# A sparse two-layer graph network on one core: the last chunk's loads before a copy, and layer 0's loop recut

## The chip, the cores and the metric

The kernel runs on one core of a Trainium2 chip. The core has five engines that work side by side, each through its own list of instructions in order: PE (matrix products), DVE (vector operations), ACT (scalar functions and copies), POOL (here it issues the gathers and scatters) and SP (here it issues plain transfers). Semaphores make one engine wait for another. Transfers of all of them run on 16 DMA engines. The metric is the device time in microseconds (us) of one execution; lower is better.

## The reference, cut to what matters

There are N = 3327 nodes with 512 features each, and a symmetric 0/1 adjacency matrix with ones on its diagonal, in which a row holds few ones. Two layers follow one another:

```python
# layer 0: attention with 4 heads of 128
feats = einsum('nf,hfo->hno', x, W)
logits = leaky(e_self[:, None] + e_neigh[None, :], 0.2)      # only where adj is 1
x = layernorm(x + relu(softmax(logits) @ feats + b))
# layer 1: a gated sum of an attention over x @ W_sa and a plain sum over x @ W_gcnb
a = exp(-leaky(s_left[:, None] + s_right[None, :], 0.01)) * adj
x = layernorm(x + sigmoid(gate_a * (a / a.sum(1)) @ (x @ W_sa) + gate_b * (adj @ (x @ W_g) + b_g)))
```

## The kernel before, in words

The kernel never forms the dense attention. It reads the adjacency matrix once, turns each row into a list of neighbours, sorts the nodes by their number of neighbours, and then gathers the feature rows of the neighbours. Nodes are worked on in tiles of 128, 26 of them: 12 in a first group, 14 in a second. `CAPS` gives the neighbours of each tile, its own node apart (14 down to 5, and 14 down to 4). The two tiles with the longest lists (`T0`, tiles 0 and 12) have a further row of shared slots, the stairs.

**Loading.** The matrix comes in seven chunks of 512 columns, the last of 256. SP issues the loads in the order of the program: 13 blocks of a chunk (`load_adj`, line 222, into 12 rotating buffers), then a chunk of x (`load_x`). Ahead of the last chunk's 13 blocks SP issues `x_rows` (line 238), a copy within HBM of the first group's x rows into `table0`, beside the place of their features, so that one gather brings a node's x and its features together. Two more copies of that kind, for the second group (`own1`, lines 989 and 990), are issued later in the program and stand next in SP's list.

For each chunk, PE sums the blocks into codes (`add_codes`, line 403), ACT takes them out of PSUM (`take_codes`), PE turns them (`turn_codes`), and DVE draws the lists from them with top-eight operations (`top_codes`, `decode`, `pick`). Between these, `features` multiplies x by the weights of layer 0 and POOL writes the rows to `table0`.

**Layer 0.** Gathers go into a ring of 42 slots (`RING`). `plan` gives each row of each tile of `order0` its slot; `gather` (line 616 through `indirect`) issues, on POOL, the gathers for which slots are free by the program's count. A gather waits for the readers of the old row in its slot. `order0` begins with tiles 11, 10, 0, 1, 2; the two first are short (6 and 7 rows). For each tile:

- `weigh_a` and `weigh_b` compute the softmax weights of its rows, on DVE and ACT. They need all its gathers.
- `attend` multiplies each row by its weights, one per head, and adds it up on PE in the accumulator `acc` by a product with the identity (line 804). Rows whose number leaves 2 after division by 3 are multiplied by ACT in four pieces (line 796), the others by DVE (line 798). From the fourth tile on (`lean`) the bias is added to row 0 on DVE (line 803); otherwise PE adds it (line 790).
- `finish` takes the accumulator, adds x (line 883, DVE), and frees the tile's slots.
- `columns1` turns the tile on PE, `columns2a` copies that on ACT, `columns2` multiplies it on PE by eight columns that layer 1 needs, `columns3` copies the result on DVE (line 839).
- `norm.add` takes statistics on DVE; for each group of up to four tiles `publish` writes the normalised rows to `table1`.

In the order of the program tiles 11 and 10 (`early`) are weighed before the last chunk's codes are summed, and multiplied and added up right after that. The other 24 tiles are in a loop. In its iteration i an engine's list holds: publishing that is due; the copy of tile i-2's turned columns; the rows of tile i, multiplied and added up, with the eight columns of tile i-2 on PE after the third row; the finishing of tile i-1, its turning and statistics; the column copy of tile i-2; two of the 14 steps that sort the second group (`sort1`) while these last; the weights of tile i+1.

**Layer 1** follows with a loop of its own over gathers from `table1`; the change doesn't touch it.

Of the kernel before, what the change touches and what calls it, by code (L numbers as in the profile page):

```python
# [14 lines left out]
P = 128  # L15
# [63 lines left out]
def sparse_pass(  # L79
# [156 lines left out]
    for i in range(len(chunks)):  # L236
        if i == len(chunks) - 1:
            x_rows = nc.sync.dma_start(twos.rearrange("(n t) w -> n t w", t=2)[:, 0, :], xo[:N0]).ins
            tc.add_to_no_dep_group("x rows", x_rows)
        load_adj(i)  # L240
        load_x(i + 2)

# [301 lines left out]
    def sort1(to, t0, t1):  # L544
# [16 lines left out]
        if t1 == n:  # L561
            by_tile = in_place[0].rearrange("p (t w) -> p t w", t=n)
            nc.vector.tensor_copy(srt[1][:, :, : S + 2], by_tile[:, :, : S + 2])
            nc.vector.tensor_copy(srt[1][:, :, S + 2 : W1].bitcast(F32), by_tile[:, :, S + 2 :])
# [34 lines left out]
    def climb(g, pool, psum):  # L599

        of = pool.tile([P, B + H], F32, tag="of", name=f"of{g}")
        nc.vector.tensor_copy(of[:, :B], srt[g][:, 0, C0 + 1 : S + 1])
        nc.vector.tensor_copy(of[:, B:], srt[g][:, 0, S + 2 : S + 2 + H].bitcast(F32))
        nc.tensor.matmul(psum, to_row, of, start=True, stop=True)
        nc.vector.tensor_mul(of[:, :B], psum[:, :B], step_of)
        id_ = pool.tile([P, 1], F32, tag="id_", name=f"id_{g}")
        nc.vector.tensor_reduce(id_, of[:, :B], AX.X, ALU.add)
        nc.vector.tensor_copy(ids2[g], id_)
        nc.vector.tensor_copy(es2[g], psum[:, B:])
# [134 lines left out]
    def weigh_a(j):  # L744
# [6 lines left out]
        if j in T0:  # L751
            logit = m0.tile([P, H], F32, tag="logit", name=f"logit{j}")
            nc.vector.tensor_add(logit, stair[j][:, F : F + H], es2[g])
            small = psx.tile([P, B * H], F32, tag="pcol", name=f"to_nodes{j}", bufs=2)
# [19 lines left out]
    def weigh_b(j):  # L774
# [5 lines left out]
        if j in T0:  # L780
            small = psx.tile([P, B * H], F32, tag="pcol", name=f"to_rows{j}", bufs=2)
            ws2[j] = to_rows(m0, small, f"n{j}", w[:, C0 + 1 :, :])

    def attend(j, lean, between):


        w = ws[j]
        acc = accs[j] = ps.tile([P, F], F32, tag="acc", name=f"acc{j}", bufs=2)
        if not lean:
            nc.tensor.matmul(acc, ident, bias0, start=True, stop=False)  # L790
        for s0, n, buf, o in got[j]:
            for s in range(s0, s0 + n):
                gv = buf[:, o + s - s0, 0:F].rearrange("p (h o) -> p h o", h=H)
                if s % 3 == 2:
# [6 lines left out]
                row = buf[:, o + s - s0, 0:F]  # L801
                if lean and s == 0:
                    nc.vector.tensor_add(row, row, bias0)
                nc.tensor.matmul(  # L804
                    acc, ident, row, start=(lean and s == 0), stop=(s == CAPS[j] and j not in T0)
                )
                if s == 2:
                    between()
        if j in T0:
# [4 lines left out]
            nc.tensor.matmul(acc, to_node, stair[j][:, 0:F], start=False, stop=True)  # L814

# [54 lines left out]
    early = order0[:2]  # L872

    def at_first():

        a, b = (CAPS[j] + 1 for j in early)
        waiting[: a + b] = waiting[1:a] + waiting[a + 1 : a + b] + [waiting[0], waiting[a]]
        for _ in range(a + b - 2):
            tc.declare_no_dep(indirect(*waiting.pop(0)[1:]), group="x rows", reason="they read rows of features only")
# [11 lines left out]
    for i in range(len(chunks)):  # L891
        if i == len(chunks) - 1:
# [5 lines left out]
            for j in early:  # L898
                weigh_a(j)
                weigh_b(j)  # L900
        add_codes(i)
        if i == len(chunks) - 1:
            for j in early:
                attend(j, False, lambda: None)
        take_codes(i)
        if i == len(chunks) - 1:
            for j in early:
                finish(j)
# [5 lines left out]
        if i == NC0 + 2:  # L914
            climb(0, p0, psl.tile([P, CH], F32, tag="pc1", name="climb0")[:, : B + H])
# [29 lines left out]
    weigh_a(order0[2])  # L945
    weigh_b(order0[2])
    ready = [[], []]
    for i in range(NT + 3):
# [3 lines left out]
        third = order0[i - 2] if 2 <= i < NT + 2 else None  # L952
        if third is not None:
            columns2a(third)
        if 2 <= i < NT:
            attend(order0[i], i >= 3, lambda: third is None or columns2(third))
        elif third is not None:
            columns2(third)
        if 0 < i <= NT:
            j = order0[i - 1]  # L960
            y = row1(j)[:, 0:F]
            if i > 2:
                finish(j)
            if not waiting:
                put_rows()
            columns1(j)
            done = norm.add(i - 1, y)
            if done:
                k0, scale, shift = done
                ready[1] = [  # L970
                    (order0[k], scale[:, k - k0 : k - k0 + 1], shift[:, k - k0 : k - k0 + 1]) for k in range(k0, i)
                ]
        if i > NT:
            put_rows()
        if 2 <= i < NT + 2:
            columns3(order0[i - 2])
        if 0 < i <= 7:
            sort1(rankis[1], 2 * i - 2, 2 * i)
        if i == 8:
            climb(1, m0, psx.tile([P, B * H], F32, tag="pcol", name="climb1", bufs=2)[:, : B + H])  # L980
# [10 lines left out]
        if 2 <= i < NT - 1:  # L991
            weigh_a(order0[i + 1])
            weigh_b(order0[i + 1])
# [658 lines left out]
```

## Time and profile before

| | |
|---|---|
| median of three runs | 940.53 us (937.54 to 941.17) |
| the profiled execution, as timed | 1068.62 us |
| its span, first to last instruction | 1066.8 us |
| mean granted clock of PE | 0.865 |
| busy PE, DVE, ACT, POOL | 814.2, 735.3, 289.0, 593.5 us |
| moved by DMA | 224.68 MB, 211 GB/s on average |

The profile is of one execution, which took longer than those without a profile; durations in it are those of that execution. A group of instructions is shown as source line, engine, operation and `out<-in` with its shape and count, then its busy time, the mean of one in ns, and how long its engine stood idle ahead of it, with what ended most of that idle time (`<-`). In stretches of the span, "clock" is the share of PE's full clock that was granted, and the DMA share is the mean busy share of the 16 DMA engines. A product of 512 columns in fp32 shows as two matmul records. "remote" or "unknown" stands where the trace shows no releaser.

### The profile page before, as it was taken

The page shows a single profiled execution, that of the slowest core. Times are in us where ns is not written, and L with a number is a line of the kernel's source. Part 1 is how long each engine was busy: PE and PEld are TensorE (multiplying, and loading weights), DVE is VectorE, ACT ScalarE, POOL GpSimd, SP SyncE. Part 2 cuts the span into 40 slices and gives each one's busy share as a digit, 9 for nine tenths or more (in the row PEclk, how much of TensorE's full clock was granted, in tenths as well). Part 3 has the DMA queues.
Part 4 walks back from the last instruction along what each step waited for, and adds up shares of the span by engine and source line. Part 5 has one row for each costly group of instructions (what it writes and reads, how often), then busy time and mean ns, then how long its engine had stood idle before and what let it go on. Part 6 is the DMA issues. An engine that isn't in the chain of part 4 may idle for free. (4 is left out here: it accounts for less than half of the span.)

```text
span 1066.8 us, 10313 instructions
## 1 busy us (share of the span) xinstructions
PE 814.2 (76%) x2518; PEld 426.4 (40%) x2518; DVE 735.3 (69%) x2100; ACT 289.0 (27%) x820; POOL 593.5 (56%) x641
## 2 busy tenths in 40 slices
PE   5698972521987877777987956639999999969993
PEld 4476751201443433333443422214444444434441
DVE  3486788407857467655756757348798998989973
ACT  1122220200424243432434422112323123232331
POOL 7511243760566666465766247765667777757611
PEclk9898995565898879788987977769999999989997
DMA  9999899991477668586676127755656666746400
GB/s 341 371 361 399 342 325 351 377 386 53 126 212 235 199 192 251 144 307 197 183 210 198 61 98 196 207 164 140 188 144 186 183 182 182 195 129 182 167 28 35
DMA packets 73349, 224.68 MB, mean 211 GB/s; under 512 B 12736, under 2 KB 16784, under 8 KB 72384
## 3 DMA queue, kind: packets, MB, share of 16 engines
q0 software_dynamic: 46368, 153.69, 48.8%
q1 hardware_dynamic: 24256, 68.13, 16.8%
q10 hardware_dynamic: 2656, 2.10, 0.6%
q8 instruction: 23, 0.38, 0.1%
q14 instruction: 46, 0.38, 0.1%
HBM read 203.02 MB, written 31.51 MB: 220 GB/s over the span
## 5 line engine op out<-in xcount | busy, mean ns | idle before, releaser
L616 POOL DMA_INDIRECT ring<-table,srt x464 | 475.2, 1024 | 265.1 <-issue 98.8
L804 PE MATMUL acc<-ring,ident 128*128 128x512 f32 x504 | 261.9, 667 | 56.6 <-ACT ring L796 18.5
L1097 DVE SCALAR_TENSOR_TENSOR sw<-ring,e,sw 128x512 f32<-128x512 f32 x226 | 169.4, 750 | 11.6 <-ACT sw L1081 4.7
L804 PEld LDWEIGHTS acc<-ring,ident 128*128 128x128 f32 x504 | 101.7, 212 | 178.8 <-issue 109.2
L1118 PE MATMUL acc<-ring,ident 128*128 128x512 f32 x264 | 126.4, 613 | 13.8 <-DMA ring<-table,srt 9.7
L372 PE MATMUL pf<-w,xc 128*128 128x260 f32 x416 | 105.3, 417 | 13.1 <-DVE w L312 13.1
L798 DVE TENSOR_TENSOR ring<-ring,w 128x512 f32<-128x512 f32 x176 | 111.3, 691 | 1.7 <-DVE w L779 1.2
L1137 PE MATMUL po<-wsa,sT 128*128 128x512 f32 x208 | 98.4, 617 | 18.5 <-ACT sT L1130 10.3
L372 PEld LDWEIGHTS pf<-w,xc 128*128 128x128 f32 x416 | 85.8, 209 | 30.1 <-DVE w L312 13.8
L1137 PE MATMUL po<-wg,sT 128*128 128x512 f32 x208 | 93.8, 593 | 0.8 <-issue 0.8
L796 ACT ACTIVATE ring<-ring,w 128x128 f32<-128x128 f32 x304 | 91.5, 389 | 0.0
L1118 PEld LDWEIGHTS acc<-ring,ident 128*128 128x128 f32 x264 | 50.7, 194 | 81.8 <-issue 54.7
L1137 PEld LDWEIGHTS po<-wsa,sT 128*128 128x128 f32 x208 | 40.9, 199 | 73.4 <-issue 59.3
L1099 DVE TENSOR_TENSOR ring<-ring 128x512 f32<-128x512 f32 x94 | 65.0, 692 | 3.2
L403 PE MATMUL pc<-at,pow 128*32 128x512 bf16 (+1 forms) x182 | 24.6, 414 | 53.0 <-DMA at<-in_adjB 24.4
L384 POOL DMA_DIRECT2D table<-row x26 | 14.3, 549 | 87.2 <-ACT st L381 84.6
L763 ACT ACTIVATE w<-w 128x40 f32<-128x40 f32 (+10 forms) x26 | 6.2, 237 | 201.5 <-DVE w L762 124.8
L1137 PEld LDWEIGHTS po<-wg,sT 128*128 128x128 f32 x208 | 39.3, 190 | 49.9 <-issue 49.7
L1130 ACT COPY sT<-pt 128x512 f32<-128x512 f32 x52 | 28.7, 587 | 102.0 <-remote 48.8
L376 ACT COPY row<-pf 128x512 f32<-128x512 f32 x26 | 15.2, 585 | 96.2 <-PE pf L372 50.6
L829 ACT COPY xt<-x1t 128x512 f32<-128x512 f32 x26 | 15.2, 584 | 94.9 <-remote 39.2
L835 PEld LDWEIGHTS pcol<-v,xt 128*128 128x128 f32 x208 | 33.1, 228 | 17.3 <-issue 14.1
(254 smaller groups left out, 941.7 us busy)
## 6 DMA issues: line engine op xcount, KB each, us to landing
at<-in_adjB SPq DMA_DIRECT2D x78, 512.0 KB
ring<-table,srt POOLq DMA_INDIRECT x464
table<-row POOLq DMA_DIRECT2D x26, 260.0 KB
xc<-in_xB SPq DMA_DIRECT2D x6, 1024.0 KB
own<-in_xo SPq DMA_DIRECT2D x1, 3640.0 KB
own<-table SPq DMA_DIRECT2D x1, 3640.0 KB
at<-in_adjL SPq DMA_DIRECT2D x13, 256.0 KB
table<-in_xo SPq DMA_DIRECT2D x1, 3120.0 KB
```

Of the source, the lines that this page charges most:

```text
L372: nc.tensor.matmul(pf[:, hh, :HC], xc[:, k, o : o + P], w0[:, k, hh, :], start=(k == 0), stop=(k == KT - 1))
L403: nc.tensor.matmul(pc[32 * c : 32 * c + 32, : nt * P], pow2[:, s, :], loaded[i, m], start=(s == 0), stop=(m + 1 not in ms or s == 3),)
L616: return nc.gpsimd.indirect_dma_start(out=out_, out_offset=None, in_=table, in_offset=bass.IndirectOffsetOnAxis(ap=ap, axis=0)).ins
L796: nc.scalar.activation(gv[:, h, :], gv[:, h, :], AF.Copy, scale=w[:, s, h : h + 1])
L798: nc.vector.tensor_tensor(gv, gv, w[:, s, :].rearrange("p (h o) -> p h o", o=1).to_broadcast([P, H, FO]), ALU.mult)
L804: nc.tensor.matmul(acc, ident, row, start=(lean and s == 0), stop=(s == CAPS[j] and j not in T0))
L835: nc.tensor.matmul(pcol, xt1[:, k, :], v1[:, k, :], start=(k == 0), stop=(k == KT - 1))
L1097: nc.vector.scalar_tensor_tensor(sw, g[:, i, 0:F], e[:, s : s + 1], sw, ALU.mult, ALU.add)
L1099: nc.vector.tensor_add(g[:, i, 0:F], g[:, i - 1, 0:F], g[:, i, 0:F])
L1118: nc.tensor.matmul(plain[j], to, row, start=(not sums_of_two and i == 0), stop=(sums_of_two and i == len(rows) - 1),)
L1130: nc.scalar.copy(sT, pt)
L1137: nc.tensor.matmul(proj[j], sT[:, k, :], wt[:, k, :], start=(half + k == 0), stop=(half + k == KT))
```

## The change

It has two parts.

The loads: `x_rows` is issued after the last chunk's loads rather than before. Tiles 11 and 10 are no longer worked on inside the last chunk. `at_first` now issues the gathers of three tiles' rows (11, 10 and 0) that hold features only, 26 of them where there were 11, and then the three tiles' own rows, which wait for the copy.

The loop: it now runs over all 26 tiles. `attend` is cut into `multiply` (DVE and ACT) and `add_up` (PE). In an iteration the list is: the products of tile i; the weights of tile i+1, if its rows fit in the ring beside those not yet freed; the sums of tile i; finishing, turning and statistics of tile i-1; the weights of i+1 if they were not yet done; the columns of tile i-2; the column copy of tile i-3; publishing; sorting. In `lean` tiles rows 0 and 1 are multiplied by four operations each, one per head, that add the bias to row 0, and row 0 to row 1; PE then adds up one row fewer. `climb`, which prepares the stairs, is in two halves an iteration apart for the second group, and small PSUM tiles have a bank of their own (`aux`).

```diff
     for i in range(len(chunks)):
-        if i == len(chunks) - 1:
-            x_rows = nc.sync.dma_start(twos.rearrange("(n t) w -> n t w", t=2)[:, 0, :], xo[:N0]).ins
-            tc.add_to_no_dep_group("x rows", x_rows)
         load_adj(i)
         load_x(i + 2)
+    x_rows = nc.sync.dma_start(twos.rearrange("(n t) w -> n t w", t=2)[:, 0, :], xo[:N0]).ins
+    tc.add_to_no_dep_group("x rows", x_rows)
...
-    def attend(j, lean, between):
+    def multiply(j, lean):
         w = ws[j]
-        acc = accs[j] = ps.tile([P, F], F32, tag="acc", name=f"acc{j}", bufs=2)
-        if not lean:
-            nc.tensor.matmul(acc, ident, bias0, start=True, stop=False)
+        below = bias0
         for s0, n, buf, o in got[j]:
             for s in range(s0, s0 + n):
-                gv = buf[:, o + s - s0, 0:F].rearrange("p (h o) -> p h o", h=H)
-                if s % 3 == 2:
+                row = buf[:, o + s - s0, 0:F]
+                gv = row.rearrange("p (h o) -> p h o", h=H)
+                if lean and s < 2:
+                    for h in range(H):
+                        part = slice(h * FO, (h + 1) * FO)
+                        nc.vector.scalar_tensor_tensor(
+                            row[:, part], row[:, part], w[:, s, h : h + 1], below[:, part], ALU.mult, ALU.add
+                        )
+                    below = row
+                elif s % 3 == 2:
...
-                row = buf[:, o + s - s0, 0:F]
-                if lean and s == 0:
-                    nc.vector.tensor_add(row, row, bias0)
-                nc.tensor.matmul(
-                    acc, ident, row, start=(lean and s == 0), stop=(s == CAPS[j] and j not in T0)
-                )
-                if s == 2:
-                    between()
...
+    def add_up(j, lean):
+        acc = accs[j] = ps.tile([P, F], F32, tag="acc", name=f"acc{j}", bufs=2)
+        rows = [(ident, buf[:, o + k, 0:F]) for _, n, buf, o in got[j] for k in range(n)]
+        rows = rows[1:] if lean else [(ident, bias0)] + rows
+        if j in T0:
+            rows.append((to_node, stair[j][:, 0:F]))
+        for k, (to, row) in enumerate(rows):
+            nc.tensor.matmul(acc, to, row, start=(k == 0), stop=(k == len(rows) - 1))
...
-    early = order0[:2]
     def at_first():
-        a, b = (CAPS[j] + 1 for j in early)
-        waiting[: a + b] = waiting[1:a] + waiting[a + 1 : a + b] + [waiting[0], waiting[a]]
-        for _ in range(a + b - 2):
-            tc.declare_no_dep(indirect(*waiting.pop(0)[1:]), group="x rows", reason="they read rows of features only")
+        whole, part, owns = [], [], []
+        for j in order0[:3]:
+            n = CAPS[j] + 1 + (j in T0)
+            whole, part, owns = whole + waiting[:n], part + waiting[1:n], owns + waiting[:1]
+            del waiting[:n]
+        waiting[:0] = owns
+        for args in part:
+            tc.declare_no_dep(indirect(*args[1:]), group="x rows", reason="they read rows of features only")
...
-    weigh_a(order0[2])
-    weigh_b(order0[2])
+    weigh(at_(0))
     ready = [[], []]
-    for i in range(NT + 3):
...
+    for i in range(NT + 4):
+        cur, nxt, done, turned_ = at_(i), at_(i + 1), at_(i - 1), at_(i - 2)
+        past = [at_(k) for k in ([i - 3] if i < NT else [i - 2]) if at_(k) is not None]
+        if i == NT:
+            past = [at_(i - 3)] + past
+        if cur is not None:
+            multiply(cur, i >= 3)
+        early = nxt is not None and (i == 0 or ends_at[nxt] - freed[0] <= RING)
+        if early:
+            weigh(nxt)
+        if cur is not None:
+            add_up(cur, i >= 3)
+        if done is not None:
+            finish(done)
+            columns1(done)
+            if not waiting:
+                put_rows()
+            norm_done = norm.add(i - 1, row1(done)[:, 0:F])
+        if nxt is not None and not early:
+            weigh(nxt)
+        if turned_ is not None:
+            columns2a(turned_)
+            columns2(turned_)
+        for j in past:
+            columns3(j)
+        for args in ready[0]:
+            publish(*args)
...
```

## The prediction

> **What bounds the kernel now.** The profiled execution has a span of 1066.8 us (1068.62 us as timed); the three runs without a profile have a median of 940.53 us. I read the page first, then stretches of the span, then the groups of instructions of layer 0, then who waits for whom. Columns of the first view: stretch, length, busy PE, weight loads, DVE, ACT, POOL (with counts), granted clock, DMA share, GB/s.
>
> ```profile
> 168.00:186.00 18.00, 2.12 (x9) 1.79 (x10) 15.83 (x70) 0.00 (x0) 7.54 (x8) 0.50 1.02 329
> 186.00:203.00 17.00, 5.04 (x28) 1.53 (x27) 13.16 (x49) 6.92 (x23) 12.53 (x13) 0.50 1.02 366
> 203.00:221.00 18.00, 16.13 (x35) 7.08 (x35) 0.13 (x1) 0.47 (x1) 13.68 (x15) 0.86 1.03 387
> 221.00:244.00 23.00, 0.24 (x1) 0.00 (x0) 1.40 (x3) 0.00 (x0) 12.80 (x14) 0.52 0.99 370
> 244.00:264.00 20.00, 4.52 (x12) 2.96 (x12) 16.54 (x70) 0.00 (x0) 0.00 (x0) 0.50 0.04 15
> 289.00:622.00 333.00, 273.10 (x757) 134.78 (x756) 211.66 (x618) 128.94 (x383) 200.92 (x204) 0.87 0.66 196
> ```
>
> The DMA engines are full until 244. From 203 to 244 DVE does almost nothing, though it still owes the last chunk's lists (244 to 264, with POOL and DMA then idle). From 289 to 622, 23 tiles of layer 0 take 14.5 us each and no engine is full: PE stands still for 60 us, DVE for 121 us, POOL for 132 us.
>
> Why the last chunk is late: SP's queue in the timeline and the waits of PE and POOL.
>
> ```profile
> 156.87 0.56 SPq L238 DMA_DIRECT2D table<-in_xo  x1
> 157.52 32.45 SPq L222 DMA_DIRECT2D at<-in_adjL  x13
> 191.00 16.10 SPq L990 DMA_DIRECT2D own<-table  x1
> 186.38 0.40 PE L403 MATMUL pc<-at,pow 128*32 128x256 bf16 x2 [16.04 <-DMA at<-in_adjL]
> 186.56 0.94 POOL L616 DMA_INDIRECT ring<-table,srt  x1 [8.72 <-DMA table<-in_xo]
> ```
>
> The chunk before had landed by 166.6; the copy of x rows takes the next 20 us, and only then do the 13 blocks of the last chunk land, some 0.73 us apart. Behind them PE sums two early tiles (203 to 219) before it turns the codes.
>
> Inside layer 0, the groups (busy us, mean ns, idle before) and one line's view:
>
> ```profile
> L616 POOL DMA_INDIRECT ring<-table,srt x464 | 475.2, 1024 | 265.1 <-issue 98.8 <-PE acc L804 34.9 <-PE acc L1118 34.8
> L804 PE MATMUL acc<-ring,ident 128*128 128x512 f32 x504 | 261.9, 667 | 56.6 <-ACT ring L796 18.5 <-DVE ring L803 18.3 <-issue 13.5
> L798 DVE TENSOR_TENSOR ring<-ring,w 128x512 f32<-128x512 f32 x176 | 111.3, 691 | 1.7 <-DVE w L779 1.2
> L803 DVE TENSOR_TENSOR ring<-ring,bias 128x512 f32<-128x512 f32 x23 | 16.1, 698 | 0.8
> L750 DVE TENSOR_TENSOR w<-ring,srt 128x36 f32<-128x36 f32 x7 | 1.4, 193 | 0.8 <-issue 0.4 <-DMA ring<-table,srt 0.2
> ```
>
> ```profile
> its engine sat idle before it (us, times) until:
>   PE acc L804: 44.6, 8
>   PE pcol L835: 20.1, 7
> ```
>
> The second is line 839, the copy of a tile's eight columns. It waits 65 us for PE, and weights and products of the next tile queue behind it on DVE; then PE waits for those (L796, L803). The weights (L750) hardly ever wait for a gather, and POOL waits 34.9 us until PE releases slots. So the loop is paced by the two engines waiting for each other, not by gathers.
>
> [...]at 221 to 244 PE, DVE and ACT stop for a releaser that it calls unknown while DMA is full[...].
>
> **The change, part by part.**
>
> *Loads.* No transfer is added. The 13 blocks follow the previous chunk: from 166.6, 13 x 0.73 = 9.5 us alone, landing by about 178 with gathers between. The x rows' copy follows on SP's queue, 20 us: landed at about 198 instead of 186.5. The two copies at lines 989 and 990 queue behind it and end near 241 as before, since the bytes are the same. POOL's queue is passed too: 26 gathers of features only instead of 11, so it is busy from 164 to 197 rather than standing 8.7 us; then three own rows (201), landed at about 208 (an own gather issued at 186.56 was used at 193.89, 7.3 us).
>
> *Early tiles.* Tiles 11 and 10 no longer run inside the last chunk. DVE ends the chunk before at 191.7 and goes straight to the last one, 19.8 us (243.98 to 263.76): first weights at 211.5, after the own rows' 208. The two tiles now cost there about 12.4 us: weights 3.6, products 5.6, finishing and statistics 3.2. Then tile 0 takes its 25 us (263.8 to 288.8) and is finished at 249 instead of 288.8: -40 us. But full DMA until 241 lies over this stretch, and the 23 us silence may simply recur in the new place. I take it as recurring: -17. Bounds: 0 (own rows 23 us later still) and -40.
>
> *Scaling with bias.* 23 tiles lose one add (L803) and two products (L798), together 0.72+0.65+0.63 = 2.0 us in the timeline, and get eight 128-wide operations. None such is in the trace. [...]L1097, dependent on itself and with the same scalar operand, starts every 0.77 us at 512 wide, [...]I take 2.3: +0.3 us, range -0.2 to +1.0, on a DVE with 121 us idle; without that cover 23 x 0.3 = 7 us. PE loses one row of two matmuls every 0.43 us: 23 x 0.86 = 20 us.
>
> *Recut.* Products of tile i, then weights of i+1, then the finishing of i-1; columns come an iteration later (i-3), so the 65 us of L839 go, because their matmuls are then an iteration old. PE's sums run as one block that lags DVE. What is late next is gathering: the 23 tiles after tile 0 need 225 gathers at 1.25 us (0.95 and the 0.30 gap, as in the timeline) = 281 us. PE needs (225-23) x 0.86 + 23 x 1.55 for columns + 13 for sorting = 222 us at full clock; DVE 211.7+7 busy, about 235 with gaps. So the stretch falls from 333 to no less than 281: -52. Loss of step between three engines with floors this close, seven iterations with 3.7 us of sorting on DVE, and a DMA share rising from 0.66 to about 0.78 make me take half: -26. The split climb, the moved sort copies and one more PSUM bank are under 1 us, hidden by DVE's idle time; the one extra iteration at the end is empty.
>
> Sum: -17 - 26 = -43, so 1068.6 becomes about 1026. Subtracted from the median this is 897, in proportion 903. I say 899.
>
> **The rivals.**
>
> *Only the start pays.* If ring and gathers already set the pace without a profile, the recut gives nothing: -17, about 923. For: 225 gathers fill 281 of 333 us. Against: L750's missing DMA waits.
>
> *Nothing moves.* Own rows under full DMA arrive 20 us later than reckoned and the loop keeps 14.5 us: 938 to 943. For: share 1.02. Against: POOL got its steady 1.25 us there.
>
> *Slower.* Weights of i+1 now stand ahead of the finishing of i-1. If they wait for gathers in most tiles, everything behind waits too: finish 0.7, statistics 0.9, columns 0.2, publishing and normalising 1.5 = 3.3 us, 1.0 for dear scaling, and PE's transposes and columns, 1.55, which hang on the finish. 5.85 x 23 = 134 us against 20 + 65 saved and 17 at the start: +32, about 970. It decides from 102/134, about 18 of 23 tiles late. Against: a ring of 42 slots holds 3.6 mean tiles, and POOL was the one to wait.
>
> *All of it.* No silence and gathers at their floor: -40 - 52, about 850.
>
> **How the numbers follow.** Forecast (870 to 915) 0.50; only the start 0.17; nothing 0.07; slower 0.16; all of it 0.10. Faster by over 0.5% is 0.50+0.17+0.10 = 0.77, within 0.5% 0.07, slower 0.16; half a per cent is about what these runs, 3.6 us apart, can tell from no change. The range runs from 862 (half of the best case left out) to 948 (most of the slow case left out). The likeliest case's own range is 870 to 915.
>
> **What would show it.** Right: no wait of PE over 5 us for the last chunk's blocks; x rows landed near 198; DVE's top-eight operations of the last chunk starting near 192; the columns' copy without waits; POOL's gap in layer 0 near its 0.30; PE's clock above 0.9 there; 23 tiles in about 307 us; 23 fewer rows on PE. Wrong: weights waiting for DMA in most tiles, a silence longer than 23 us after the last chunk, per-head operations above 0.4 us, or a loop still at 14.5 us a tile.

## The result, and the profile after

The kernel after takes **993.02 us** (990.83 to 993.70) against 939.19 us for the kernel before beside it: a ratio of 1.0583, 95% interval 1.0551 to 1.0614. It is slower by 5.8%; the prediction said 899 us and faster. The ratios and this range leave out executions in a slower state, such as a fourth one of the kernel after that took 1200.35 us at a granted clock of 0.639.

On some chips the kernel before takes about 936 us, on others about 1074, with stalls whose releaser the trace calls remote (at line 883 alone 36.8 us of them in the first profile); the profile ahead of the prediction (1068.62 us) is of the second kind and its median (940.53) of the first, so each run below is compared with the kernel before measured beside it. The profile of the kernel after is of the first kind: a span of 990.2 us, 992.33 us as timed. The kernel before was therefore profiled again on a chip of the first kind (`before_again`: span 934.8, 936.86 us as timed), and that is the one to hold beside it. It also shows that the first profile's length does not come from profiling.

**The start.** The kernel after, stretches of the span (columns as in the first view ahead of the prediction):

```profile
203.00:221.00 18.00, 13.87 (x25) 6.63 (x26) 13.64 (x39) 6.62 (x22) 13.35 (x13) 0.55 1.02 378
221.00:244.00 23.00, 20.46 (x52) 9.84 (x51) 19.74 (x55) 13.28 (x45) 18.57 (x13) 0.93 0.80 290
...
289.00:560.00 271.00, 195.62 (x555) 100.75 (x554) 168.37 (x581) 103.27 (x310) 216.55 (x179) 0.83 0.72 214
```

and the kernel before in its second profile:

```profile
203.00:221.00 18.00, 15.94 (x36) 6.99 (x35) 2.58 (x7) 0.47 (x1) 13.44 (x15) 0.86 1.03 383
221.00:244.00 23.00, 5.74 (x17) 4.03 (x18) 17.71 (x74) 1.11 (x4) 9.86 (x11) 0.51 0.82 325
```

The silence of DVE from 203 to 244 is gone; on this kind of chip the kernel before had only its first half. Of the kernel after, SP's queue, one wait of PE and one of POOL, and the first weights on DVE, from its timeline:

```profile
153.70 19.33 SPq L222 DMA_DIRECT2D at<-in_adjL  x13
173.09 1.33 SPq L239 DMA_DIRECT2D table<-in_xo  x1
...
181.62 0.40 PE L402 MATMUL pc<-at,pow 128*32 128x256 bf16 x2 [1.34 <-DMA at<-in_adjL]
...
202.13 0.96 POOL L625 DMA_INDIRECT ring<-table,srt  x1 [8.22 <-DMA table<-in_xo]
...
211.01 0.18 DVE L759 TENSOR_TENSOR w<-ring,srt 128x24 f32<-128x24 f32 x1 [1.39 <-DMA ring<-table,srt]
```

PE no longer waits 16 us for the last chunk's blocks, POOL takes up the gathers that need the x rows at 202.1, the first weights start at 211.0. Up to here nearly all went as forecast; only POOL stands still for 8.22 us ahead of the x rows, where it was to be busy until they land. The last stretch of the first fence does not: POOL is busy 216.55 us with 179 transfers and has some 0.30 us between two, 216.55 + 179 x 0.30 = 270 of 271 us. PE and DVE are busy for 195.62 and 168.37 us of it. Layer 0 is paced by POOL.

**Layer 0 beside the kernel before.** The groups of the kernel after:

```profile
L625 POOL DMA_INDIRECT ring<-table,srt x464 | 534.2, 1151 | 160.2 <-issue 69.6 <-DMA ring<-table,srt 34.8 <-PE acc L829 10.1
L829 PE MATMUL acc<-ring,ident 128*128 128x512 f32 x458 | 225.5, 650 | 27.3 <-DVE ring L804 16.9 <-DMA ring<-table,srt 10.4
...
L812 DVE TENSOR_TENSOR ring<-ring,w 128x512 f32<-128x512 f32 x130 | 80.4, 684 | 0.0
L804 DVE SCALAR_TENSOR_TENSOR ring<-ring,w,bias 128x128 f32<-128x128 f32 x92 | 26.1, 346 | 0.0
L804 DVE SCALAR_TENSOR_TENSOR ring<-ring,w 128x128 f32<-128x128 f32 x92 | 26.0, 344 | 0.0
...
L759 DVE TENSOR_TENSOR w<-ring,srt 128x36 f32<-128x36 f32 (+11 forms) x31 | 5.9, 194 | 100.8 <-DMA ring<-table,srt 81.7 <-DMA ring<-table,ids 11.8 <-issue 7.3
```

and of the kernel before in its second profile:

```profile
L616 POOL DMA_INDIRECT ring<-table,srt x464 | 475.5, 1025 | 173.1 <-issue 65.0 <-DMA ring<-table,srt 33.5 <-PE acc L804 25.2
...
L798 DVE TENSOR_TENSOR ring<-ring,w 128x512 f32<-128x512 f32 x176 | 111.9, 694 | 0.6
L803 DVE TENSOR_TENSOR ring<-ring,bias 128x512 f32<-128x512 f32 x23 | 16.0, 694 | 0.8
```

with its stretch of layer 0, from the same 289 to its last gather:

```profile
289.00:513.00 224.00, 206.14 (x636) 102.27 (x635) 180.44 (x523) 108.86 (x322) 170.99 (x175) 0.96 0.83 254
```

The same 464 gathers are 534.2 - 475.5 = 58.7 us longer on POOL, 1151 ns each instead of 1025. The kernel before was paced by POOL too: 170.99 + 175 x 0.30 = 223.5 of 224 us. On DVE the scaling costs 80.4 + 26.1 + 26.0 = 132.5 us against 111.9 + 16.0 = 127.9: 4.6 us, 0.2 a tile.

The column copy, which waited 65 us in the first profile, waits 15.0 us for PE in the second, and in the kernel after 2.0 (view of line 852):

```profile
its engine sat idle before it (us, times) until:
  PE pcol L848: 2.0, 1
```

**One tile.** The first tile with per-head operations in the kernel after, DVE and then POOL in the timeline:

```profile
241.49 1.13 DVE L804 SCALAR_TENSOR_TENSOR ring<-ring,w,bias 128x128 f32<-128x128 f32 x4
242.54 1.13 DVE L804 SCALAR_TENSOR_TENSOR ring<-ring,w 128x128 f32<-128x128 f32 x4
243.59 4.30 DVE L812 TENSOR_TENSOR ring<-ring,w 128x512 f32<-128x512 f32 x7
...
241.94 0.98 POOL L625 DMA_INDIRECT ring<-table,srt  x1 [0.30 <-DVE ring L804]
243.22 5.49 POOL L625 DMA_INDIRECT ring<-table,srt  x1 [0.30 <-issue]
```

and the same tile in the kernel before, second profile:

```profile
258.84 0.69 DVE L798 TENSOR_TENSOR ring<-ring,w 128x512 f32<-128x512 f32 x1
259.56 0.69 DVE L803 TENSOR_TENSOR ring<-ring,bias 128x512 f32<-128x512 f32 x1
260.17 5.03 DVE L798 TENSOR_TENSOR ring<-ring,w 128x512 f32<-128x512 f32 x8
...
259.32 1.03 POOL L616 DMA_INDIRECT ring<-table,srt  x1 [0.30 <-issue]
260.65 1.02 POOL L616 DMA_INDIRECT ring<-table,srt  x1 [0.30 <-PE acc L804]
261.98 0.95 POOL L616 DMA_INDIRECT ring<-table,srt  x1 [0.30 <-issue]
263.23 0.95 POOL L616 DMA_INDIRECT ring<-table,srt  x1 [0.30 <-PE acc L804]
```

In the kernel after one gather lasts 5.49 us: the run of products is closed to it. It ends at 248.71, 0.82 us behind the end of the run of products (243.59 + 4.30 = 247.89). In the kernel before, gathers start every 1.33 or 1.25 us through a run that is longer still. What differs ahead of the run is a gap: L803 adds the bias to the row that L798 has just written, so it starts 0.72 us after L798, where the run starts 0.61 us after L803. The per-head operations leave no such gap.

In layer 0 of the kernel after, 23 of 254 gathers last over 1.6 us; what they take beyond 0.95 us is 67.8 us in all. Two of the 23, with 8.4 us, lie in the first three tiles, which have no per-head operations. In the second profile of the kernel before there is none.

**Where the 55.4 us are.** Spans: 990.2 - 934.8 = 55.4. Gathering for layer 0 begins at 161.6 (163.3 before) and ends at 559.8 (512.0): 47.8 us. From there to the first gather of layer 1 (595.7 and 540.3) it takes 35.9 us instead of 28.3: 7.7 us. Layer 1 takes 394.5 us in both.

### The profile page after: what moved, and what is told of

Same layout as the page of the kernel before. It is cut to its first block, busy times and chain, and to the rows that moved or that the text cites. A ratio compares the mean times of both kernels' runs of the same rounds, so it can differ in the third digit from the quotient of the medians.

```text
span 990.2 us, 10297 instructions
## 1 busy us (share of the span) xinstructions
PE 781.7 (79%) x2472; PEld 414.6 (42%) x2472; DVE 733.9 (74%) x2215; ACT 286.3 (29%) x820; POOL 661.3 (67%) x641
## 3 DMA queue, kind: packets, MB, share of 16 engines
q0 software_dynamic: 46368, 153.69, 52.4%
## 5 line engine op out<-in xcount | busy, mean ns | idle before, releaser
L625 POOL DMA_INDIRECT ring<-table,srt x464 | 534.2, 1151 | 160.2 <-issue 69.6
L829 PE MATMUL acc<-ring,ident 128*128 128x512 f32 x458 | 225.5, 650 | 27.3 <-DVE ring L804 16.9
L829 PEld LDWEIGHTS acc<-ring,ident 128*128 128x128 f32 x458 | 94.3, 211 | 145.6 <-issue 90.8
L1138 PE MATMUL acc<-ring,ident 128*128 128x512 f32 x264 | 127.0, 609 | 22.2 <-DVE ring L1119 11.5
L1157 PE MATMUL po<-wsa,sT 128*128 128x512 f32 x208 | 93.6, 593 | 0.3 <-ACT sT L1150 0.3
L1138 PEld LDWEIGHTS acc<-ring,ident 128*128 128x128 f32 x264 | 49.4, 192 | 92.8 <-issue 44.7
L759 DVE TENSOR_TENSOR w<-ring,srt 128x36 f32<-128x36 f32 (+11 forms) x31 | 5.9, 194 | 100.8 <-DMA ring<-table,srt 81.7
L812 DVE TENSOR_TENSOR ring<-ring,w 128x512 f32<-128x512 f32 x130 | 80.4, 684 | 0.0
L1189 ACT ACTIVATE za<-za 128x512 f32<-128x512 f32 x26 | 16.4, 631 | 163.1 <-DVE za L1187 163.1
L1157 PEld LDWEIGHTS po<-wsa,sT 128*128 128x128 f32 x208 | 39.4, 190 | 49.8 <-issue 47.8
L1157 PEld LDWEIGHTS po<-wg,sT 128*128 128x128 f32 x208 | 39.4, 190 | 48.8 <-issue 47.8
## 6 DMA issues: line engine op xcount, KB each, us to landing
at<-in_adjB SPq DMA_DIRECT2D x78, 512.0 KB, 11.8
table<-in_xo SPq DMA_DIRECT2D x1, 3120.0 KB, 28.3
```

Source lines behind the costliest of these rows:

```text
L625: return nc.gpsimd.indirect_dma_start(out=out_, out_offset=None, in_=table, in_offset=bass.IndirectOffsetOnAxis(ap=ap, axis=0)).ins
L812: nc.vector.tensor_tensor(gv, gv, w[:, s, :].rearrange("p (h o) -> p h o", o=1).to_broadcast([P, H, FO]), ALU.mult)
L829: nc.tensor.matmul(acc, to, row, start=(k == 0), stop=(k == len(rows) - 1))
L1138: nc.tensor.matmul(plain[j], to, row, start=(not sums_of_two and i == 0), stop=(sums_of_two and i == len(rows) - 1),)
L1157: nc.tensor.matmul(proj[j], sT[:, k, :], wt[:, k, :], start=(half + k == 0), stop=(half + k == KT))
```

## The experiments

The theories at the start: **stretched gathers** (products on DVE hold POOL up), **order** (the prediction's slower rival: weights of i+1 ahead of the finishing of i-1), **per-head operations** as such, **the loads' order**.

### The kernel before once more, and the parts one at a time

`before_again` is the kernel before, unchanged.

> The kernel before, profiled once more, since its profile (1066.8 us) is 13% longer than its unprofiled time (939). If that profile is typical, this one is again above 1050, with layer 0 at 14.5 us per tile. If it was an odd execution, this one has a span near 938, layer 1 takes about 395 us (as in the kernel after) and layer 0's last gather is issued near 505 instead of 580. Gathers theory: POOL's long gathers (over 1.6 us) then total under 20 us, against 69 us in the kernel after. Weights theory: L750 waits for DMA under 20 us, against 82 us.

936.86 us, no gather over 1.6 us, weights (L750) waiting 2.3 us for gathers. The first profile was not like the runs that it was taken to explain. Layer 0's last gather ends at 512.0, close to the 505 expected.

`after_plain_scaling`:

```diff
-                if lean and s < 2:
-                    ...  # four operations, one per head
-                elif s % 3 == 2:
+                if s % 3 == 2:
...
+                if lean and s == 0:
+                    nc.vector.tensor_add(row, row, bias0)
...
-        rows = rows[1:] if lean else [(ident, bias0)] + rows
+        rows = rows if lean else [(ident, bias0)] + rows
```

> The kernel after with rows 0 and 1 scaled by whole-row products and the bias added by its own operation, as before; loads and order as after. If the per-head operations cause the loss, this is near 940 or below. If the order (weights ahead of the finishing) or the gathers behind the products cause it, this stays at 985 to 1005, the long gathers still total 50 us or more.

937.62 us; ratio to before (935.89) 1.0011, interval 0.9995 to 1.0027. The whole loss is gone; loads and order, which stay, together neither gain nor lose.

`before_per_head` puts only the per-head operations into the kernel before (rows 0 and 1 of `lean` tiles, one product with the identity fewer).

> The kernel before with only the per-head operations for rows 0 and 1 of 23 tiles (one matmul less per tile), loads and order as before. If they cause the loss, this takes 980 or more. If they are as cheap as in the kernel after (1.13 us for a row), this takes 930 to 945.

986.89 us; ratio 1.0542 (1.0498 to 1.0586). So the loss comes with the per-head operations, in either loop, and the order is not its cause. But they take DVE no longer than reckoned: eight take 52.4 / 23 = 2.3 us of busy time, and 22 gathers are stretched by 53.0 us in all.

`after_x_rows_first`:

```diff
     for i in range(len(chunks)):
+        if i == len(chunks) - 1:
+            x_rows = nc.sync.dma_start(...)
         load_adj(i)
         load_x(i + 2)
-    x_rows = nc.sync.dma_start(...)
```

> The kernel after with the copy of x rows ahead of the last chunk's loads again, all else as after. If the moved load is worth the 17 us of the prediction, this takes 1005 to 1015. If the load order causes the loss (x rows late, so that tile 0 starts late), this falls below 970. If the loop's pace decides from POOL's 254 gathers, the start counts only through when gathering starts: within 10 us of 993.

1018.92 us; ratio 1.0884 (1.0838 to 1.0931): 0.0884 - 0.0583 = 0.030, some 28 us, above the 17 of the prediction and against the last theory's "within 10". The trace shows how: with the first tiles worked on only after the last chunk's lists, which are late again, no slot comes free, and POOL stands still for 29.69 us behind its gather at 208.95, until ACT has copied the first tile's own row (L782). The new loop needs the moved loads; that is not the same as the loads being a gain.

### What stretches a gather

Three kernels differ only in what stands ahead of the run of products. They are the kernel after, and `after_bubble` and `after_no_bubble`, each with one more line behind row 1's per-head operations (the memory for its result apart):

```diff
                     below = row
+                    if s == 1:    # after_bubble: reads the row just written
+                        nc.vector.tensor_tensor(scratch[0][:, 0:1], row[:, F - 1 : F], row[:, F - 2 : F - 1], ALU.add)
+                    if s == 1:    # after_no_bubble: reads the bias only
+                        nc.vector.tensor_tensor(scratch[0][:, 0:1], bias0[:, 0:1], bias0[:, 1:2], ALU.add)
```

> The kernel after with one tensor_tensor of 128x1 per tile between the per-head operations and the run of whole-row products; it reads the row just written, so DVE waits for its own result before the run starts. Lock theory (a run that starts without a gap behind a scalar_tensor_tensor keeps GpSimd out until it ends): 23 small operations cost DVE some 4 us, yet gathers are no longer stretched (long gathers under 15 us in all) and the time falls to 930 to 945. If the stretching comes from the products themselves or from the per-head operations' own traffic, it stays at 990 to 1000.

> The same small tensor_tensor in the same place, reading only the bias, so that nothing waits for it. If the gap is what lets GpSimd in, the gathers stay stretched and this takes 985 to 1000. If it is the kind of the operation ahead of the run (scalar_tensor_tensor or tensor_tensor), this falls to 930 to 945 as well.

With the gap: 938.40 us, ratio 1.0030 (1.0006 to 1.0053). Without it: 984.29 us, 1.0524 (1.0483 to 1.0565). The two have the same operations; one waits for its own row. "Lock" in the expectations is the author's name for a supposed hold of POOL until the end of a run; gathers that end just after a run are what the traces show, and no lock as such. `after_bubble`, the same tile, DVE and POOL:

```profile
241.04 1.13 DVE L809 SCALAR_TENSOR_TENSOR ring<-ring,w 128x128 f32<-128x128 f32 x4
242.21 0.16 DVE L814 TENSOR_TENSOR scratch<-ring 128x1 f32<-128x1 f32 x1
242.29 4.38 DVE L819 TENSOR_TENSOR ring<-ring,w 128x512 f32<-128x512 f32 x7
...
242.51 1.27 POOL L625 DMA_INDIRECT ring<-table,srt  x1 [0.30 <-DVE scratch L814]
244.09 0.95 POOL L625 DMA_INDIRECT ring<-table,srt  x1 [0.30 <-PE acc L836]
```

Against 243.22 + 5.49 in the kernel after, a gather that starts inside the run now takes 1.27 us, and the next 0.95. The run itself takes 4.38 us instead of 4.30 for seven products: DVE pays 0.08 us a tile for letting POOL in.

`after_per_head_last` scales the same rows by the same operations, but behind the others (`every = every[2:] + every[:2]`), and sums them last.

> The kernel after with the per-head rows 0 and 1 scaled behind the other rows of a tile instead of ahead of them; the sums take them last too. The same operations, in another order. Lock theory: runs that follow a copy or a small operation are free, those that follow the sorting's L553-like operations (iterations up to 7) are not: 930 to 960, long gathers under 30 us. If the per-head operations cost by being there, it stays at 985 to 1000.

955.23 us, 1.0223 (1.0187 to 1.0259). Four of the first tiles with per-head operations still show a gather of 3.46 to 5.23 us, and those runs follow the sorting's 420-wide scalar_tensor_tensor (L553) without a gap (a fifth such run is open); later runs follow a copy or a small operation, and gathers pass: they are open. As expected, the place decides and not the presence of the operations.

`plain_one_per_head` takes the whole-row kernel and puts one idle scalar_tensor_tensor between the bias' addition and the run.

> The kernel with whole-row scaling (937.6 us) and, per tile, one per-head-shaped scalar_tensor_tensor of 128x128 on a scratch tile, put between the bias' addition and the run of products; its result is used by nobody. It costs DVE 0.26 us a tile, 6 us in all. Lock theory: gathers stretch again in nearly all 23 tiles and the time rises to 975 to 1000. Without the lock it takes 937 to 945.

942.37 us, 1.0066 (1.0031 to 1.0101): a **miss**. The run follows a scalar_tensor_tensor without a gap, and yet it is open:

```profile
257.58 0.69 DVE L814 TENSOR_TENSOR ring<-ring,bias 128x512 f32<-128x512 f32 x1
258.19 0.34 DVE L815 SCALAR_TENSOR_TENSOR scratch<-scratch,w,bias 128x128 f32<-128x128 f32 x1
258.45 4.38 DVE L810 TENSOR_TENSOR ring<-ring,w 128x512 f32<-128x512 f32 x7
...
258.67 1.28 POOL L625 DMA_INDIRECT ring<-table,srt  x1 [0.30 <-issue]
260.26 0.95 POOL L625 DMA_INDIRECT ring<-table,srt  x1 [0.30 <-issue]
```

The gap lies two operations ahead of the run here, ahead of L814, and the run is open all the same. So it isn't the kind of the operation directly ahead. Nor is a gap somewhere ahead enough, as a tile of `before_per_head` shows:

```profile
272.99 0.21 DVE L779 TENSOR_TENSOR w<-w,den 128x48 f32<-128x48 f32 x1
273.24 1.14 DVE L799 SCALAR_TENSOR_TENSOR ring<-ring,w,bias 128x128 f32<-128x128 f32 x4
274.29 1.13 DVE L799 SCALAR_TENSOR_TENSOR ring<-ring,w 128x128 f32<-128x128 f32 x4
275.34 3.69 DVE L807 TENSOR_TENSOR ring<-ring,w 128x512 f32<-128x512 f32 x6
...
275.50 4.36 POOL L616 DMA_INDIRECT ring<-table,srt  x1 [0.30 <-DVE ring L799]
```

The per-head operations wait for the weights of L779 (0.25 us from start to start, though L779 takes 0.21) and so begin behind a gap; the eight and the run follow without a break, and the run is closed. In these kernels a gap opened the run when it lay directly ahead of it (a gather of 1.27 us in `after_bubble`), or when only copies and small operations, or the bias' addition and one scalar_tensor_tensor (1.28 us here), stood between. With eight per-head operations between (4.36 us), or nearly always with L553 (3.46 to 5.23 us), it did not. What makes the difference was not found.

All these together, with what their gathers for layer 0 over 1.6 us took beyond 0.95 us, and the end of gathering for layer 0. The kernel before beside `after` took 939.2 us, beside the others 935.4 to 935.9:

| kernel | us | long gathers | beyond 0.95, us | last gather ends |
|---|---|---|---|---|
| before_again | 936.9 | 0 | 0 | 512.0 |
| after_plain_scaling | 937.6 | 5 | 12.2 | 504.7 |
| after_bubble | 938.4 | 4 | 10.8 | 505.0 |
| plain_one_per_head | 942.4 | 3 | 10.0 | 512.0 |
| after_per_head_last | 955.2 | 11 | 27.4 | 524.5 |
| after_no_bubble | 984.3 | 24 | 60.8 | 551.7 |
| before_per_head | 986.9 | 22 | 53.0 | 558.8 |
| after | 993.0 | 23 | 67.8 | 559.8 |

From `after_bubble` to `after` the gathers grow by 57.0 us and the time by 54.6 (by 53.8 - 3.0 = 50.8 if each is first compared with the kernel before beside it); from `after_bubble` to `after_per_head_last` by 16.6 and 16.8. So, on this kind of chip, nearly each microsecond that a gather stands still is one of the kernel's.

### Both inputs in SBUF?

A whole-row product takes both its inputs from SBUF, the row (`ring`) and the weights (`w`), and the row numbers of a gather stand in SBUF too (`srt`). The author's guess was that the second input is what holds the gathers. If so, products that take the weights from PSUM let them pass without any gap. `after_weights_in_psum` does that, at one small copy more per tile (other small tiles move into the same PSUM bank):

```diff
+        wps[j] = bank[0][:, 256 : 256 + (S + 1) * H].rearrange("p (s h) -> p s h", h=H)   # a PSUM bank
+        nc.vector.tensor_copy(wps[j][:, :c], w[:, :c])
...
-                        gv, gv, w[:, s, :].rearrange(...).to_broadcast([P, H, FO]), ALU.mult
+                        gv, gv, wps[j][:, s, :].rearrange(...).to_broadcast([P, H, FO]), ALU.mult
```

> The kernel after, whose whole-row products (L812) take the weights from a copy in PSUM instead of SBUF; one copy of 128 x (4 columns a row) more per tile on DVE, about 0.2 us, 5 us in all; no gap is added ahead of the run. If gathers stand still because both inputs of the products come from SBUF, they pass: long gathers under 10 us in all and 930 to 945. If any unbroken run on DVE locks GpSimd out, whatever its inputs, it stays at 985 to 1000.

> The kernel after, whose whole-row products take the weights from a copy in PSUM (one small copy more per tile on DVE), measured beside a kernel before of about 936 us. If gathers stand still because both inputs of the products come from SBUF, they pass although no gap was added: long gathers under 10 us in all and 928 to 945. If any unbroken run on DVE locks GpSimd out, whatever its inputs, it stays at 985 to 1000.

> The weights of the whole-row products in PSUM, once more. Beside a kernel before of about 936 us: 928 to 945, since its gathers were seen to pass in every run of products; with the two gathers of the first tiles freed too, 930 is the likeliest. Beside a kernel before of about 1074 us: 1040 to 1070, faster by up to 3% or no difference.

All three were run on chips where the kernel before takes 1073 to 1075 us, so the figures near 936 in the expectations were not put to the test. Gathers are stretched on such a chip too: 17 of them in the kernel after (`after_again`, below). An eight-product run straight behind per-head operations:

```profile
424.46 4.86 DVE L815 TENSOR_TENSOR ring<-ring,bank 128x512 f32<-128x512 f32 x8
...
424.62 0.95 POOL L625 DMA_INDIRECT ring<-table,srt  x1 [0.30 <-PE x1t L839]
425.87 0.95 POOL L625 DMA_INDIRECT ring<-table,srt  x1 [0.30 <-issue]
427.12 0.95 POOL L625 DMA_INDIRECT ring<-table,srt  x1 [0.30 <-DVE ring L815]
```

Gathers at their 1.25 us, with no gap directly ahead of the run. In layer 0 no gather lasted over 1.6 us in the first of the three and two lasted 1.79 or 1.80 us in each of the others; those two began within the per-head operations, which still read two inputs from SBUF. Of the 17 in the kernel after the longest took 7.71 us. So in these kernels it is the products' second input from SBUF that holds the gathers: with it from PSUM no gather that started within a run of products lasted over 1.6 us. By what means it holds them no trace shows.

Times: 1053.84 us against 1073.89, ratio 0.9752 (0.9661 to 0.9842); 1068.07 against 1073.32, not told apart; 1070.98 against 1075.46, ratio 0.9821 (0.9745 to 0.9897). The two ratios rest on two of four and three of twelve executions of the kernel, and the last two medians lie 0.4% apart, so a gain over the kernel before is likely there rather than shown. It is faster than the kernel after on the same chip (1097.71). Beside 936 it was not measured.

`after_bubble_in_mid_run` puts the waiting operation behind the second product of the run instead of ahead of the first.

> The kernel after with the small waiting tensor_tensor not ahead of the run but behind its second product (row 4), so that two products run locked and the rest behind a gap. If the gap lets the waiting gather in and the rest of the run then stays open, the long gathers fall to about 2 us each (under 25 us in all) and the time to 940 to 955. If only the start of the run decides, gathers stay stretched to the run's end: 985 or more.

> The kernel after with the small waiting tensor_tensor behind the second product of the run (row 4), measured beside a kernel before of about 936 us. If the gap lets the waiting gather in and the rest of the run then stays open, a stretched gather takes 1.6 to 2.5 us (excess about 1 us a tile, under 35 us with the first tiles) and the time is 940 to 960. If only the start of the run decides, gathers stay stretched to the run's end: 985 or more.

```profile
345.83 1.29 DVE L817 TENSOR_TENSOR ring<-ring,w 128x512 f32<-128x512 f32 x2
347.15 0.16 DVE L821 TENSOR_TENSOR scratch<-ring 128x1 f32<-128x1 f32 x1
347.23 1.89 DVE L817 TENSOR_TENSOR ring<-ring,w 128x512 f32<-128x512 f32 x3
...
345.46 2.48 POOL L625 DMA_INDIRECT ring<-table,srt  x1 [0.30 <-PE sorted L557]
348.24 1.09 POOL L625 DMA_INDIRECT ring<-table,srt  x1 [0.31 <-issue]
```

The gather waits for two products, gets in at the gap and ends at 347.94, 0.82 us behind the two products' end (347.12); the next one takes 1.09 us within the rest of the run. So here a gap within a run opened the products behind it. The long gathers are down to 15 with 21.4 us in all, and 11 with 16.6 in the second of these runs. The times, 1077.07 against 1073.89 and 1072.70 against 1073.32 (1.0036, 0.9870 to 1.0202), do not tell the kernels apart.

### The loads alone, gaps everywhere, and the change on the other chips

> The kernel before with only the last chunk's loads put ahead of the x rows' copy. The prediction's step on the loads would give up to 17 us (919 to 925), with the two early tiles' own rows about 12 us later. If gathering paces layer 0 from its first gather at 163, POOL's waits at 176 and 232 to 252 (24 us in the kernel before) are all that can be won: 920 to 940. If the own rows of the early tiles come too late for the last chunk, slower: up to 955.

> The kernel before with only the last chunk's loads ahead of the x rows' copy, measured beside a kernel before of about 936 us. The prediction's step on the loads gives up to 17 us: 919 to 925. If gathering paces layer 0, only POOL's waits at 176 and 232 to 252 (24 us) can be won, and the early tiles' own rows come some 12 us later: 925 to 945.

1076.96 us against 1073.89 (ratio 1.0060, 0.9993 to 1.0128) and 1074.81 against 1073.32 (1.0109, 0.9963 to 1.0254). With the early tiles inside the last chunk no gain of the moved loads alone shows there; beside 936 this was not measured.

`after_bubbles_everywhere` adds two small operations, one waiting for the other, ahead of the first three tiles' products too.

> The kernel with the gap ahead of the run (938.4 us) and two small tensor_tensor operations, the second waiting for the first, ahead of the products of the first three tiles too, whose runs follow the sorting's scalar_tensor_tensor and stretch two gathers by 9 us together. If gathering paces layer 0, these 9 us come back in part: 928 to 936, below both kernels. If the start of the loop is covered, 936 to 940.

> The gap ahead of the run in all 26 tiles, the first three included, measured beside a kernel before of about 936 us. The gap in 23 tiles gave 938.4. If gathering paces layer 0, the 9 us of the two gathers that were still stretched come back: 928 to 936. If not, 936 to 941.

1075.65 us against 1073.89, and 1050.71 against 1073.32 (0.9897, 0.9788 to 1.0007): inconclusive. In its traces no gather of the first three tiles is stretched any more. Whether the 9 us come back beside 936 stays open.

> The kernel after itself, beside the same kernel before. Beside 936 us: 985 to 997, 6% slower, as first measured. Beside 1074 us, where other stalls set the pace of layer 0 (20 us and more for each of several stretches in which engines wait for a releaser that the trace calls remote), the stretched gathers cost less or nothing: 1070 to 1100; if they cost as much as elsewhere, 1120 to 1135.

The kernel after beside 1075.46 us takes 1097.71: ratio 1.0275 (1.0168 to 1.0381); the medians are 22 us apart, by the ratio it is some 29. Seventeen gathers are stretched by 53.2 us, against 23 and 67.8 on the other chip, and about half of it reaches the end. The sign is the same. That the rest is hidden because POOL there also waits for other engines (10.5 us for releasers called remote between 260 and 590) is argued, not shown.

## Why the prediction was wrong

The forecast of 899 us and the 993 measured lie 94 us apart. Some 54 of them are a loss that the forecast put at 0.3 us a tile and took as hidden; the other 40 or so are gains that did not come.

**The first step that failed: "Scaling with bias", "I take 2.3: +0.3 us", hidden by "a DVE with 121 us idle".** The 2.3 us for eight operations were an estimate of the author's, since no such operation stood in the trace. As a price on DVE they were right: the eight end 2.18 us after they begin (241.49 to 243.67; each lasts 0.35 us, where 2.3 / 8 is 0.29, but they overlap), and the sum is 0.2 us a tile. What the step left out is what the removed instruction did for another engine. The wait of L803 for its own engine's last result left a gap of 0.1 us per tile, and through it POOL got into the run of products. Without the gap, layer 0's gathers stand still for 67.8 us; `after_bubble`, which puts the gap back, leaves 10.8 and is 54.6 us faster: 55 / 23 = 2.4 us a tile, not 0.3. The operation was priced only on the engine that runs it.

**The second step that failed: "the loop is paced by the two engines waiting for each other, not by gathers", with "225 gathers at 1.25 us", 281 us, as a floor to fall to.** The 1.25 us holds only while DVE lets POOL in; in the kernel after, a gather and its gap take (216.55 + 179 x 0.30) / 179 = 1.51 us on average, scatters included. And without the stalls of the first profile the kernel before was at that floor already (223.5 of 224 us). So the recut's -26 could not exist there. PE's lighter load could not pay either: 458 records in `after_bubble`, 504 in `after_plain_scaling`, 938.4 and 937.6 us.

**The base of the sum.** "1068.6 becomes about 1026. Subtracted from the median this is 897" rests on 65 us of waits and a silence of 41 us in an execution 128 us longer than the runs. On a chip where the kernel takes 936 us, the column copy waits 15 us, and DVE is back at work between 221 and 244. The size of the possible gain was that of another situation; the 128 us should have been explained first.

**The loads: landings nearly right, worth wrong.** The last block at 184.2 (said: by about 178), x rows at 202.1 (198), first weights at 211.0 (211.5), tile 0 finished at 251.3 (249). A head start was there as well, for a while: in `after_bubble` the fourth tile's run starts at 242.3, in the kernel before at 260.2. That these 17.9 us are near the forecast's 17 is luck, since the 17 were 40 less a silence of 23 us (221 to 244) that this kind of chip does not have. Then the wait for gathers uses the head start up: the last gather ends at 505.0 instead of 512.0, and from there to layer 1 the recut loop takes 35.8 us instead of 28.3, since POOL waits 10.62 and 4.03 us for the publishing of the last tiles where it waited 6.55. 505.0 + 35.8 = 540.8 against 512.0 + 28.3 = 540.3: nothing is left. That the longer tail comes from the columns being an iteration later is argued, not tried.

**The slower rival** ended on the right side for a wrong reason. Its sign was there (weights wait 100.8 us, 81.7 of them for gathers of features, L759), but as a consequence: with the same order `after_bubble` loses nothing, though its weights still wait 43.4 us, 18.8 of them for these. The rival "only the start pays" had the recut right: "ring and gathers already set the pace without a profile", so that the recut gives nothing; the 17 us that it left to the start were used up as told above. "Nothing moves" names the time of `after_plain_scaling` (938 to 943; 937.6), but not its reason: the own rows were there some 3 us later than reckoned (211.0 against 208), not 20.

**The signals named.** Right: no wait of PE over 5 us for the last blocks, the columns' copy all but without waits (2.0 us), POOL's gap of 0.30, fewer rows on PE (46 records fewer). Wrong: PE's clock was 0.83 where over 0.9 was forecast (PE had work for 195.62 of 271 us), and weights waited for DMA. Per-head operations cost under 0.4 us (0.35), so that the one signal set for this part stayed silent while it did all the harm.

## What to carry to other kernels

Before an operation is replaced by a cheaper or equal one, look at what its waits give to other engines: here a dependent operation's short gap on DVE was what let POOL's gathers in. Where gathers are issued by POOL beside long unbroken runs of two-input products on DVE, compare the longest gather with the shortest (here 5.49 and some 0.95 us); if the longest end a fixed time after the run (here 0.82 us), try a dependent operation directly ahead of the run (here 938.40 us with its gap, 984.29 without), or one input in PSUM (here 17 long gathers, and then none or two). And where the profiled execution is far from the runs, settle which bound the runs have before summing gains from its waits.

## What the runs showed of the hardware

- A gather that stood still ended 0.82 us after the run that held it (248.71 and 247.89; 347.94 and 347.12). In the kernel after it is 0.81 to 0.97 us for runs of two to eleven operations. A gather that nothing held took some 0.95 us, so the hold would be near its beginning, an estimate from these figures.
- An open run and a closed one differ in pace: seven products take 4.38 us open (`after_bubble`) and 4.30 closed (the kernel after), (4.38 - 4.30) / 6 = 13 ns more per product; with weights in PSUM it is 4.26 (`weights_in_psum_3`, where gathers of 0.94 and 0.95 us start within the run).
- One gap of 0.1 us directly ahead of a run opened all of it: eight products of 128x512 in the tile of `before_again` (260.17 to 265.20, with gathers of 0.95 to 1.02 us). A gap ahead of eight per-head operations did not open the run behind them (`before_per_head`, 4.36 us). Why a run stays open or closed to its end, and why runs differ in it, was not found.
- The same program differs by 15% between chips (936 and 1074 us). Waits for a releaser that the trace calls remote stand in the profiles of the second kind only (at line 883 two with 36.8 us in the first profile, none in `before_again`); what causes them was not found.
